# Matmuls on constants in the light slots of a pair-attention stage

## The chip, the cores and the metric

The kernel runs on one core of a Trainium2 chip. Such a core has a matrix engine (TensorE, PE in the profile), VectorE (DVE), ScalarE (ACT) and GpSimd (POOL), and a queue that issues transfers (SyncE, SP). The metric is the time of one execution on the device in microseconds (us); a figure for a kernel is the median of several runs. Lower is better.

## What is computed

Two transformer layers on `x` of shape (4, 1024, 256), in float32, each with adaptive layer norms and gates from a small modulation network. The first layer has an RWKV-like recurrence and a mixture of 8 experts. The second has an attention over all pairs of tokens and a gated feed-forward network. Cut to the attention and the network of the second layer:

```python
q = jnp.einsum('bnc,ac->bna', X, Wq)
k = jnp.einsum('bnc,ac->bna', X, Wk)
Vy = jnp.einsum('bnc,dc->bnd', X, Wy_w) + Wy_b
e = jax.nn.relu(_rho_signed_sqrt(q[:, :, None, :] + k[:, None, :, :]))
scores = jnp.einsum('bija,a->bij', e, Wphi)
m = jnp.max(scores, axis=-1, keepdims=True)
ex = jnp.exp(scores - m)
denom = jnp.sum(ex, axis=-1)
part1 = jnp.einsum('bij,bjc->bic', ex, Vy)
Ew = jnp.einsum('bij,bija->bia', ex, e)
part2 = jnp.einsum('bia,ca->bic', Ew, We_w) + We_b * denom[..., None]
return (part1 + part2) / (denom[..., None] + EPS_DEN)
...
h = jax.nn.silu(_tlin(x, w1_w, w1_s)) * _tlin(x, w2_w, w2_s)
h = jax.nn.gelu(_tlin(h, h1_w, h1_s), approximate=False)
h = jax.nn.gelu(_tlin(h, h2_w, h2_s), approximate=False)
return _tlin(h, w3_w, w3_s)
```

`e` has 4 x 1024 x 1024 x 64 elements: for every pair of tokens 64 roots, which are used twice, once for the scores and once, weighted, for `Ew`.

## The kernel before

The program has two stages. `first_layer` runs the first layer; `pair_attention` runs the second, together with what is left of the first (`first_rest`) and with the feed-forward network. The change is in `pair_attention`.

The attention works on blocks of 32 queries: 128 blocks `n`, 32 for each of the four sequences. A block has 8 pairs of tiles (`p` from 0 to 7); a tile holds 128 x 1024 elements of `e`. A pair goes through these steps:

- `begin(p)` takes a buffer from a ring of 14 (`RING`) and, for some halves, has GpSimd add the query to the keys and cut at zero (L1402, L1407);
- `pair(p)`: VectorE or ScalarE adds the other halves (L1416, L1427), ScalarE takes the root of both (L1428), and TensorE multiplies them by the weights of the scores into the block's bank `sc` (L1432), 8 matmuls on four groups of 32 columns;
- later, when the block's scores are complete, `weigh(p, h)`: VectorE multiplies the roots by the spread exponentials and sums them (L1478). This ends the use of the ring's buffer.

In between, once a block: `top` (the maximum on VectorE, L1442, and two small matmuls, L1445), `exps` (L1449, L1451), `spread` (8 matmuls, two times, L1458) and `turn` (L1465).

The order is written out by hand. The main loop runs over blocks and their 8 pairs; one turn of it is called a slot here. In a slot, VectorE weighs pair `p` of the current block, then `work(ROOM[p])` gives other work a place, and then `begin` and `make` start the pairs 13 or 14 places ahead, until the scores' matmuls of one more pair have been issued. Every engine works its instructions off in the order in which they were issued.

The other work is held in two lists of generators: `tasks` (`finish`, the end of the attention for every four blocks) and `stream` (`first_rest`, then for every 256 tokens `dense`, the feed-forward network; and `prepare`, keys and values of the next sequence). A generator issues a few instructions and yields how many matmuls it has used; the room of a slot, `ROOM[p]`, is 3 to 6. A bare `yield` ends the slot for that list and reports nothing. Steps with a bare `yield` after matmuls are the transposes of `normed` (L943) and `finish` (L1491), and the projections of `prepare` (L988, L1002, L1022, L1025). The matmuls of the feed-forward network (L1263, L1333, L1354) report themselves.

The results of the other work go to two PSUM banks (`bank`, tag `"g"`); `banks[0]` counts the free ones. A bank that VectorE is to read is kept for two slots (`LATE`): `later` notes the reading instruction, `tick` at the beginning of `work` issues it when it is due and frees the bank.

`ident` is a 128 x 128 unit matrix, `pick` a constant of 128 x 512 used by `spread`, and `wsel` holds the scores' weights between columns of zeros; `wsel[:, 0, 0:1]` is a column of zeros. `made` counts the pairs whose scores have been issued, `N` is 128.

Of the kernel before, what the change touches and what calls it, by code (L numbers as in the profile page):

```python
# [14 lines left out]
P = 128  # L15
# [16 lines left out]
PREP = 12  # L32
ROOM = (4, 6, 6, 6, 6, 4, 3, 6)
LATE = 2
ADDS = ('ap', 'pp', 'pp', 'dp', 'pp', 'ap', 'dp', 'ap')
FIRST_ON_SCALAR = 6
LEAD = 2
# [6 lines left out]
@with_exitstack  # L44
def block_kernel(ctx: ExitStack, tc: tile.TileContext, a, out):
    nc = tc.nc
    keep = ctx.enter_context(tc.tile_pool(name="keep", bufs=1))


    kept = ctx.enter_context(tc.tile_pool(name="kept", bufs=1, space=DRAM))  # L50
    link = {
        "x1": [kept.tile([U, C], F32, tag=f"x1_{j}", name=f"x1_{j}") for j in range(B * T // U)],
        "x2": [kept.tile([FB, C], F32, tag=f"x2_{j}", name=f"x2_{j}") for j in range(B * T // FB)],
        "gates": [kept.tile([1, 2, B, C], F32, tag=f"gates{j}", name=f"gates{j}") for j in range(2)],
        "brow": kept.tile([1, C], F32, tag="brow", name="brow"),
        "yg": kept.tile([P, 4, U], F32, tag="yg", name="yg"),
        "qd": kept.tile([T, 64], F32, tag="qd0", name="qd0"),
        "nd": kept.tile([64, T], F32, tag="nd0", name="nd0"),
        "kd": kept.tile([8, P, T], F32, tag="kd0", name="kd0"),
        "vd": kept.tile([T, C + 1], F32, tag="vd0", name="vd0"),  # L60
    }

    ident = keep.tile([P, P], F32, tag="ident", name="ident")
    nc.scalar.dma_start(ident, a["ident"])
    cols = [keep.tile([P, 6, 2, B], F32, tag=f"mcols{i}", name=f"mcols{i}") for i in range(2)]
    seen = keep.tile([P, NE], F32, tag="seen", name="seen")
    link["qt"] = [keep.tile([P, 64, 8], F32, tag=f"qt{i}", name=f"qt{i}") for i in range(2)]
    link["wsel"] = [keep.tile([P, n], F32, tag=f"wsel{n}", name=f"wsel{n}") for n in (16, 8)]
    nc.gpsimd.memset(seen, 0.0)
    first_layer(tc, a, link, cols, seen, ident)  # L70
    pair_attention(tc, a, link, out, cols, seen, ident)
# [763 lines left out]
def pair_attention(tc, a, link, out, cols_of, seen, ident):  # L835
# [10 lines left out]
    nc = tc.nc  # L846
# [3 lines left out]
    with tc.tile_pool(name="at_k", bufs=1) as pk, tc.tile_pool(name="at_w", bufs=1) as wp, tc.tile_pool(  # L850
# [24 lines left out]
        wsel = wp.tile([P, 8, 48], F32, tag="wsel", name="wsel")  # L875
# [5 lines left out]
        pick = wp.tile([P, 2, 2, P], F32, tag="pick", name="pick")  # L881
# [168 lines left out]
        def used(j, i):  # L1050
            held.pop(j * ALL + i)
# [3 lines left out]
        banks, late = [2], []  # L1055

        def bank(shape, name):
            banks[0] -= 1
            return pg.tile(shape, F32, tag="g", name=name)

        def later(n, f):
            late.append([n, f])

        def tick():
            for x in late:
                x[0] -= 1
            while late and late[0][0] <= 0:
                late.pop(0)[1]()
                banks[0] += 1
# [174 lines left out]
        def gate(j, m):  # L1244
# [9 lines left out]
            scale = fs[:, m : m + 2, 0:1].to_broadcast([P, 2, FB])  # L1254
            later(LATE, lambda: nc.vector.tensor_tensor(to, ps, scale, ALU.mult))
            yield 4
# [22 lines left out]
        def dense(j):  # L1279
# [15 lines left out]
            def up(ps, m):  # L1295
                for h in range(2):
                    g = two[:, 4 + m + h, :] if m < 4 else one[:, m + h, :]
                    nc.vector.scalar_tensor_tensor(
                        one[:, m + h, :], ps[:, h, :], fs[:, m + h, 1:2], g, ALU.mult, ALU.mult
                    )  # L1300

            for m in range(0, 8, 2):
# [4 lines left out]
                if m % 4 == 2:  # L1307
                    used(j, W2 + m // 4)
                later(LATE, lambda ps=ps, m=m: up(ps, m))
                yield 4  # L1310
# [3 lines left out]
            for li, base, of, to in ((2, H1, one, two), (3, H2, two, one)):  # L1314

                def hidden(ps, m):
                    nc.vector.tensor_tensor(  # L1317
                        to[:, m : m + 2, :], ps, fs[:, m : m + 2, li : li + 1].to_broadcast([P, 2, FB]), ALU.mult
                    )
# [4 lines left out]
                for m in range(0, 8, 2):  # L1324
# [5 lines left out]
                    for h in range(2):  # L1330
# [7 lines left out]
                        used(j, base + m + h)  # L1338
                    later(LATE, lambda ps=ps, m=m: hidden(ps, m))
                    yield 2  # L1340
# [26 lines left out]

            later(LATE, last)
            yield 2
# [11 lines left out]
        class Block:  # L1381
# [9 lines left out]
            def adder(self, i):  # L1391
                return ADDS[i // 2][i % 2]

# [3 lines left out]
            def begin(self, p):  # L1397
                self.s[p] = ring.tile([P, 2, T], F32, tag="s", name="s")
                mine = [h for h in range(2) if self.n and self.adder(2 * p + h) == "p"]
                for h in mine:  # L1400
                    i = 2 * p + h
                    nc.gpsimd.tensor_scalar(  # L1402
                        self.s[p][:, h, :], kB[self.b][i % 8], 1.0, self.query(i), ALU.mult, ALU.add
                    )
                if mine:
                    both = self.s[p][:, mine[0] : mine[-1] + 1, :]
                    nc.gpsimd.tensor_scalar(both, both, FLT_MAX, 0.0, ALU.min, ALU.max)  # L1407
# [152 lines left out]
        N = B * NB  # L1560
        blocks = {0: Block(0)}
# [4 lines left out]
        def work(room):  # L1566


            tick()
            turns[0] += 1  # L1570
            if issues and turns[0] % 2:
                issues.pop(0)()
            for of in (tasks, stream):
                while of and room > 0:
                    got = next(of[0], self_done)
                    if got is self_done:
                        of.pop(0)
                    elif got is None:
                        break
                    else:  # L1580
                        room -= got

        def begin():
            nonlocal begun
# [29 lines left out]
        for n in range(N):  # L1614
            cur = blocks.pop(n)
            ew = ews[n // 4 % 2]
            if n % 4 == 0:
                exT = p2.tile([P, 4, 2, P], F32, tag="exT", name="exT")
            nxt = n + 1 < N
            if n % NB == PREP and n // NB + 1 < B:  # L1620
                stream.insert(min(1 + (follower() in heads), len(stream)), prepare(n // NB + 1))
            for p in range(8):
                if p == 0:
                    cur.spread(1)
                    cur.turn()
                if p == 2:
                    cur.turned(exT)
                cur.weigh(p, 0, ew)
                if made < 8 * N:
                    blocks[made // 8].adds(made % 8)  # L1630
                cur.weigh(p, 1, ew)
                if nxt and p == 5:
                    blocks[n + 1].top()
                if nxt and p == 6:
                    blocks[n + 1].exps()
                    blocks[n + 1].spread(0)
                work(ROOM[p])
                while begun <= 8 * n + p + ahead[0]:
                    begin()
                    make()  # L1640
            if n % 4 == 3:
                tasks.append(finish(n, ew, exT))
        while tasks or stream:
            work(16)
            switch()
# [101 lines left out]
```

## Time and profile before

| | us |
|---|---|
| median of 3 runs | 4834.72 |
| lowest and highest run | 4834.62, 4846.67 |
| profiled execution, whole time | 4844.85 |
| its span, first to last instruction | 4843.1 |
| first score matmul of the attention | 1092 |
| last score matmul of the attention | 4668 |
| mean granted TensorE clock | 0.915 of full |

The span is the time between the first and the last instruction of the profiled execution; 1.75 us lie around it. A page of the profile gives for every group of equal instructions the line, the engine, what is written and read, the shape and the count, then the busy time and the mean duration of one, then the idle time just ahead of them and what ended most of it. The row of the granted clock shows, in 40 slices of the span, how fast TensorE was allowed to run, in tenths. Views of a stretch show the busy time of the engines between two times, and the list of waits shows who waited for whom: total, times, longest. ACT's and DVE's rows are one record for one instruction; a float32 matmul shows as two records.

### The profile page before, as it was taken

The numbers are of one execution on the slowest core, as the hardware profiler recorded it, in microseconds if no ns is written. First come the engines' busy times: TensorE is split into PE (matmuls) and PEld (weight loads), VectorE is DVE, ScalarE is ACT, GpSimd is POOL, SyncE is SP. The second block draws the span as 40 slices with busy tenths as digits, with TensorE's granted clock in tenths as the row PEclk, the third lists the DMA queues.
The fourth block names the chain that finished last, engine by engine and source line by source line (L and its number), as shares of the span: only waits on it lengthen the run. The fifth ranks groups of instructions, "written<-read, shape, count | busy, mean of one in ns | idle before, by whom it ended". The sixth has DMA issues, their size and how long they took to land. (4 is left out here: it accounts for less than half of the span.)

```text
span 4843.1 us, 76620 instructions
## 1 busy us (share of the span) xinstructions
PE 4253.5 (88%) x28714; PEld 2423.4 (50%) x28714; DVE 3881.2 (80%) x6834; ACT 3316.7 (68%) x3183; POOL 3573.9 (74%) x2942
## 2 busy tenths in 40 slices
PE   6899999986888889899897889898889899998888
PEld 1233333433335446555564556555446555555567
DVE  5899999767898888778877878878788878878771
ACT  2333233227888898778878878888788888878851
POOL 3544444337899898889888888888898888888840
PEclk8799999987889889999998999999899999999999
DMA  4344333441112123322222332222223322222223
GB/s 137 91 120 118 107 112 108 128 140 34 33 63 68 63 73 102 105 93 81 79 86 56 109 108 83 85 79 81 66 82 105 106 86 83 77 77 75 78 86 116
DMA packets 256965, 433.16 MB, mean 89 GB/s; under 512 B 71897, under 2 KB 142737, under 8 KB 256337
## 3 DMA queue, kind: packets, MB, share of 16 engines
q1 hardware_dynamic: 253520, 425.76, 28.3%
q8 instruction: 226, 3.70, 0.3%
q10 hardware_dynamic: 2880, 1.98, 0.1%
q14 instruction: 147, 1.20, 0.1%
q0 software_dynamic: 192, 0.52, 0.0%
HBM read 403.99 MB, written 40.93 MB: 92 GB/s over the span
## 5 line engine op out<-in xcount | busy, mean ns | idle before, releaser
L1478 DVE CUSTOM_DVE_ANT_0 s<-s,xb 128x1024 f32<-128x1024 f32 x2048 | 2393.1, 1213 | 63.9 <-PE xb L1458 47.1
L1428 ACT ACTIVATE s<-s 128x2048 f32<-128x2048 f32 x1024 | 1928.6, 1908 | 174.1 <-POOL s L1407 104.6
L1402 POOL TENSOR_SCALAR s<-kB,qt 128x1024 f32<-128x1024 f32 x1397 | 1600.0, 1151 | 281.8 <-DVE ew L1478 108.4
L1407 POOL TENSOR_SCALAR s<-s 128x1024 f32<-128x1024 f32 x1016 | 1421.4, 1399 | 89.1
L1432 PE MATMUL sc<-s,wsel 128*32 128x256 f32 x16384 | 1169.6, 411 | 332.8 <-ACT s L1428 331.6
L1333 PE MATMUL ff_ps<-wide,fw 128*128 128x256 f32 x4096 | 999.1, 393 | 25.1 <-ACT wide L1375 23.7
L1432 PEld LDWEIGHTS sc<-s,wsel 128*32 128x32 f32 x16384 | 456.7, 114 | 903.2 <-ACT s L1428 500.4
L1333 PEld LDWEIGHTS ff_ps<-wide,fw 128*128 128x128 f32 x4096 | 762.8, 193 | 231.3 <-issue 102.5
L741 POOL TENSOR_TENSOR kv<-vb,out_k 128x512 f32<-128x512 f32 x256 | 324.0, 1274 | 244.0 <-DVE state L809 167.4
L1427 ACT ACTIVATE s<-kB,qt 128x1024 f32<-128x1024 f32 x387 | 439.9, 1137 | 18.6 <-DMA kB<-kd 18.1
L616 PE MATMUL e_ps<-wd,hid 128*128 128x512 f32 x896 | 417.8, 613 | 7.0 <-DVE acc L599 4.5
L1458 PE MATMUL xb<-ex,pick 64*128 64x256 f32 x2048 | 320.8, 436 | 46.2 <-ACT ex L1451 46.0
L809 DVE TENSOR_TENSOR_SCAN state<-dec,carry,kv 128x512 f32<-128x512 f32 x256 | 326.2, 1274 | 23.4 <-ACT dec L796 17.5
L616 PEld LDWEIGHTS e_ps<-wd,hid 128*128 128x128 f32 x896 | 170.9, 196 | 233.1 <-issue 219.2
L1416 DVE TENSOR_SCALAR s<-kB,qt 128x1024 f32<-128x1024 f32 x264 | 285.9, 1085 | 0.0
L1263 PE MATMUL ff_ps<-wide,fw 128*128 128x256 f32 x1024 | 268.0, 411 | 17.7 <-DMA fw<-in_ffw_dram 17.0
L1458 PEld LDWEIGHTS xb<-ex,pick 64*128 64x128 f32 x2048 | 193.2, 204 | 180.2 <-ACT ex L1451 80.0
L1317 DVE TENSOR_TENSOR wide<-ff_ps,ffn_s 128x512 f32<-128x512 f32 x128 | 88.0, 687 | 212.2 <-PE ff_ps L1333 212.2
L1442 DVE TENSOR_REDUCE sc<-sc 128x1 f32<-128x256 f32 x128 | 55.1, 431 | 249.0 <-PE sc L1432 248.4
L801 ACT COPY carry<-state 128x1 f32<-128x1 f32 x255 | 47.9, 188 | 295.6 <-DVE state L809 295.3
L1263 PEld LDWEIGHTS ff_ps<-wide,fw 128*128 128x128 f32 x1024 | 200.2, 204 | 79.7 <-issue 35.9
L1451 ACT ACTIVATE ex<-sc,neg 128x256 f32<-128x256 f32 x128 | 60.7, 474 | 254.0 <-DVE neg L1449 252.6
(254 smaller groups left out, 4155.1 us busy)
## 6 DMA issues: line engine op xcount, KB each, us to landing
fw<-in_ffw_dram SPq DMA_DIRECT2D x361, 512.0 KB
vb<-vd SPq DMA_DIRECT2D x1024, 64.0 KB
lent<-vd SPq DMA_DIRECT2D x64, 514.0 KB
wd<-in_w_down_dram SPq DMA_DIRECT2D x28, 1024.0 KB
kB<-kd SPq DMA_DIRECT2D x32, 512.0 KB
lent<-in_We_dram SPq DMA_DIRECT2D x32, 512.0 KB
kd<-nd SPq DMA_DIRECT2D x24, 512.0 KB
vd<-out_v SPq DMA_DIRECT2D x8, 512.0 KB
```

Of the source, the lines that this page charges most:

```text
L616: nc.tensor.matmul(ps, hid[:, k, t * P : (t + 1) * P], wd[:, k, :], start=k == 0, stop=k == HID // P - 1)
L741: nc.gpsimd.tensor_mul(kv, vb[:, g % 2, :], ready[u]["k"][:, n // HN, :])
L809: nc.vector.tensor_tensor_scan(s[:, 1 : U + 1], dec, kv, c, ALU.mult, ALU.add)
L1263: nc.tensor.matmul(ps[:, h, :], w[:, k, o : o + P], hT[:, k, :], start=k == 0, stop=k == 1)
L1333: nc.tensor.matmul(ps[:, h, :], w[:, k * P : (k + 1) * P], of[:, k, :], start=k == 0, stop=k == 7)
L1402: nc.gpsimd.tensor_scalar(self.s[p][:, h, :], kB[self.b][i % 8], 1.0, self.query(i), ALU.mult, ALU.add)
L1407: nc.gpsimd.tensor_scalar(both, both, FLT_MAX, 0.0, ALU.min, ALU.max)
L1427: nc.scalar.activation(t[:, h, :], kB[self.b][i % 8], AF.Relu, bias=self.query(i))
L1428: nc.scalar.activation(t, t, AF.Sqrt, bias=EPS_RHO)
L1432: nc.tensor.matmul(self.sc[32 * j : 32 * j + 32, 0:256], wsel[:, g, 16 * (1 - s) : 16 * (1 - s) + 32], t[:, h, 256 * j : 256 * (j + 1)], s ...
L1458: nc.tensor.matmul(xb[:, 256 * j : 256 * (j + 1)], pick[q, j % 2, s, :], self.ex[q, :], start=True, stop=True)
L1478: nc.vector.tensor_tensor_reduce(t[:, h, :], t[:, h, :], self.xb[s], 1.0, 0.0, ALU.mult, ALU.add, ew[:, self.n % 4, col : col + 1])
```

## The change

A constant `LEAST = 2` is added. `work` notes at its start how much room would be left after two matmuls. After the other work has had its turn, if less than two matmuls were reported, and scores are still to be made, it issues as many matmuls as are missing:

- with a free bank, into this bank: unit matrix times 256 columns of `pick`; the result is not read, and the bank is free again at once;
- without one, into the bank of the block whose scores are being made, if at least one of its pairs has been issued: unit matrix times zeros, added to the scores;
- without either, none.

They stand in TensorE's order after the other work of the slot and ahead of the next pair's scores. The result of the kernel is the same.

```diff
 LATE = 2
+LEAST = 2
 ADDS = ('ap', 'pp', 'pp', 'dp', 'pp', 'ap', 'dp', 'ap')
...
         def work(room):
 
 
+            least = room - LEAST
             tick()
             turns[0] += 1
...
                     else:
                         room -= got
+            if made < 8 * N and room > least:
+                rhs = pick.rearrange("p j s m -> p (j s m)")[:, 0:256]
+                if banks[0]:
+                    ps = bank([P, 256], "idle")
+                    for _ in range(room - least):
+                        nc.tensor.matmul(ps, ident, rhs, start=True, stop=True)
+                    banks[0] += 1
+                elif made % 8:
+                    nothing = wsel[:, 0, 0:1].to_broadcast([P, 256])
+                    for _ in range(room - least):
+                        nc.tensor.matmul(blocks[made // 8].sc[:, 0:256], ident, nothing, start=False, stop=False)
```

## The prediction, made before the changed kernel was run

> **What bounds the kernel now.** I read the page first (span, shares, the row of the granted clock, the costliest groups).
>
> ```profile
> span 4843.1 us, 76620 instructions
> ...
> PE 4253.5 (88%) x28714; PEld 2423.4 (50%) x28714; DVE 3881.2 (80%) x6834; ACT 3316.7 (68%) x3183; POOL 3573.9 (74%) x2942
> ...
> PEclk8799999987889889999998999999899999999999
> ...
> L1432 PE MATMUL sc<-s,wsel 128*32 128x256 f32 x16384 | 1169.6, 411 | 332.8 <-ACT s L1428 331.6
> L1333 PE MATMUL ff_ps<-wide,fw 128*128 128x256 f32 x4096 | 999.1, 393 | 25.1 <-ACT wide L1375 23.7
> ```
>
> No engine is full over the span, and the clock stands at 0.9 or below in many slices. L1432 shows 16384 records for 8192 matmuls in the code: a float32 matmul is two records. The change acts in the pair attention only, from 1092 us (first score matmul) to 4668 us (last). So I took that stretch by itself, then its waits, first VectorE's and then TensorE's.
>
> ```profile
> 1092.00:4668.00 3576.00, 3123.26 (x25366) 1902.67 (x25365) 2940.76 (x5334) 2979.99 (x2258) 3102.59 (x2528) 0.91 0.25 79
> ```
>
> ```profile
> DVE sc L1442 <- PE sc L1432: 248.4, 78, 8.6
> DVE wide L1317 <- PE ff_ps L1333: 119.3, 41, 5.4
> DVE neg L1449 <- PE sc L1445: 82.9, 68, 8.8
> ```
>
> ```profile
> PE sc L1432 <- ACT s L1428: 331.6, 211, 8.4
> ```
>
> The columns of the stretch are PE, PEld, DVE, ACT, POOL busy. VectorE idles 3576 - 2941 = 635 us, and 590 us of that, summed over all its waits in the stretch, ends on TensorE. TensorE idles 453 us (3576 - 3123), 332 of it for ScalarE's roots. So neither runs alone: in heavy slots TensorE is behind and VectorE waits; in light ones TensorE catches up and then starves. One heavy place (TensorE, then VectorE's wait):
>
> ```profile
> 2643.16 1.07 PE L1432 MATMUL sc<-s,wsel 128*32 128x256 f32 x16
> 2644.16 1.13 PE L1022 MATMUL vy_ps<-lent,wide 128*128 128x256 f32 x4
> 2645.22 0.69 PE L1025 MATMUL vy_ps<-lent,part 1*128 1x256 f32 x2
> 2645.85 1.13 PE L1022 MATMUL vy_ps<-lent,wide 128*128 128x256 f32 x4
> 2646.91 0.69 PE L1025 MATMUL vy_ps<-lent,part 1*128 1x256 f32 x2
> 2647.53 1.07 PE L1432 MATMUL sc<-s,wsel 128*32 128x256 f32 x16
> ```
>
> ```profile
> 2653.11 0.43 DVE L1442 TENSOR_REDUCE sc<-sc 128x1 f32<-128x256 f32 x1 [8.59 <-PE sc L1432]
> ```
>
> TensorE goes without a gap, 4.37 us from pair to pair, and VectorE pays 8.59 us at the block's maximum.
>
> **The clock.** TensorE's busy time in stretches of 3.4 us, with the granted clock next to it:
>
> ```profile
> 2583.50:2587.00 3.50, 3.25 (x34) 0.99 0.00 0
> 2587.00:2590.40 3.40, 1.06 (x16) 0.99 0.00 0
> 2590.40:2593.80 3.40, 2.40 (x21) 0.50 0.00 0
> 2597.20:2600.60 3.40, 1.16 (x16) 0.50 0.00 0
> ```
>
> After a stretch with one score pair alone (1.06 of 3.4 us) the clock is 0.50, and the pair then takes 1.93 us instead of 1.07. Over all such stretches of this stage: of 865 at full clock 89 were followed by half clock, and 81 of the 89 had a busy share under 0.48; of the 776 not followed by it only 6 did. Half clock lasts 614 us of the 3576, but VectorE's waits on TensorE lie in it for 93 us only. The other 497 us are at full clock: a backlog of work, which no clock removes.
>
> The Trainium skill, "TensorE: Matmul & The Clock Gate", section "Why this matters for your kernels", warns of idle gaps over about 3 us between bursts. This trace is stricter: the drop above follows a longest gap of 2.59 us. By the page's rule, only the 22 gaps of the stage over 3.41 us could matter, most added matmuls would keep nothing awake, and the sum below would stand near 4,950 us (an estimate from that rule).
>
> **The change, part by part.** It removes and moves nothing: in the built order the sequences of VectorE, ScalarE, GpSimd and SP are as long as before (6568, 2666, 2764 and 551 rows), no DMA is added, and no queue is passed. On TensorE it adds 368 groups of two matmuls, 315 into a spare bank and 53 adding zeros to the scores. Each stands just before a pair's score matmuls.
>
> *Price of a group.* Shape 128x256 with 128 columns of weights, as L1333. Twelve such records stand from 2504.44 to 2507.22 us, 0.232 us each; a group is four records, 0.93 us. A row with poorer weight loading, the two records of L1025 in 0.63 us, would make it 1.26. I take 0.93, the same shape. 368 x 0.93 = 342 us more TensorE work.
>
> *Where it falls.* I gave each group the pair behind it and read TensorE's idle time ahead of that pair in the trace. 125 groups have 0.93 us or more, 43 have 0.15 to 0.93, and 200 have none. So 140 us go into idle time on the spot, and 202 us push the work behind them. The cause: the code counts what steps report in `yield`, not matmuls. In 69 of the groups the slot already carries matmuls that report nothing (L943, L988, L1002, L1022, L1491). Seven such groups lie between 2626 and 2652 us, six of them on top of the heavy slots shown. Another 151 are in truly empty slots that TensorE enters late.
>
> *What reaches the end.* I walked the trace: each group adds 0.93 us of lateness, each idle time of TensorE takes off its own length, and each VectorE wait ended by TensorE turns what is left into delay. 222 us vanish in later idle time, and 121 us become longer VectorE waits, in 100 places. Bounds: 0, if the 453 us of idle took all; 202, if everything without idle on the spot counted. I take 121, since the walk decides it place by place. The cover is TensorE's wait for ScalarE; without it, all 342 us would show.
>
> *What the clock gives back.* Adding the groups' time to the 89 low stretches lifts 52 over 0.48; they lead 382 of the 614 us at half clock. TensorE's busy time there is twice what full clock needs, an excess of 147 us. The same walk with the sign turned (credit lost where TensorE idles anyway, used where VectorE waits on it) leaves 61 us. Bounds: 0, and 93, all of VectorE's waits in half clock. I take 61.
>
> *Bank waits.* The bank must be free: 83 of the groups' first matmuls wait for a VectorE reader, 27 for a ScalarE one. Behind a waiting group stand the next score pair and all of TensorE; VectorE's maximum (L1442) waits for that. Where TensorE is late the reader is done; where it is early it would idle anyway. I take 0; the other end is 83 times one eviction (L1317, 0.69 us): 57 us.
>
> *Sum.* +121 - 61 = +60 us. The profiled execution, 4844.85 us (span 4843.1 and 1.75 around it), would become 4905; it lies 10.1 us over the median of the runs, 4834.72, so the forecast is 4895 us.
>
> **The rivals.** One: it gets faster. The groups fall into idle time and the clock stays up. For it: 125 groups have full cover, and 52 stretches should be mended. It decides if fewer than 66 of the 368 groups' time ends on the path (61 / 0.93); with none, 4834.7 - 61 = 4774, at best 4742 with 93. Against it: 200 groups without cover, and the 497 us of waits at full clock. Chance 0.15. Two: cost and gain meet within 0.3% (14.5 us, about what a measurement of this kernel can tell from no change), 4820 to 4849; about two thirds of the walk's delay would have to be slack. Chance 0.10. Three: the clock is not held, that is, it doesn't do what it is meant to: 4834.7 + 121 = 4956. For it: 32 low stretches have no group in them, and pairs come irregularly against fixed stretches. Against it: 1.07 + 0.93 = 2.0 of 3.4 us is 0.59, over 0.48. Chance 0.12. Four: bank waits stop TensorE's queue: 4895 + 57 = 4952. Against it: the readers are issued before. Chance 0.08.
>
> **How the numbers follow.** The forecast (15 to 105 us slower) has 0.55. Slower in all: 0.55 + 0.12 + 0.08 = 0.75; same 0.10; faster 0.15. The likeliest case's own range is 4850 to 4940. The range to hold 8 in 10 takes in no change below and a clock that isn't held above: 4822 to 4957.
>
> **What would show it.** Right: TensorE's busy time in the attention up by 150 us or more; half clock in it down from 614 to about 250 us, and the mean clock up from 0.91; its wait for ScalarE at L1432 down by half from 332 us; VectorE's waits at the maximum (248 us) and on evictions up although the clock is better; longest around the key projections (L1022). First layer (to 1092 us) and tail (after 4668) unchanged. Wrong: VectorE's waits on TensorE falling under 590 us, which means that lateness is swallowed and the clock's gain stays; half clock near 614 us, which means rival three; added matmuls shown waiting for VectorE by tens of us, which means rival four.

## The result, and the profile after

The changed kernel takes 4912.60 us (median of 4 runs, 4907.74 to 4922.57) against 4840.69 us of the kernel before (4 runs, 4834.62 to 4846.71): ratio 1.0151, 95% interval 1.0132 to 1.0171, so 72 us slower. The profiled execution took 4908.31 us.

The page of the kernel after, the rows that answer to those of before (line numbers are one higher up to L1566; the added matmuls are L1589 into a bank and L1594 as zeros):

```profile
span 4906.5 us, 79572 instructions
...
PE 4488.6 (91%) x30186; PEld 2597.7 (53%) x30186; DVE 3873.9 (79%) x6834; ACT 3315.7 (68%) x3183; POOL 3576.2 (73%) x2942
...
PEclk8799999988999999999999999999999999999999
...
L1433 PE MATMUL sc<-s,wsel 128*32 128x256 f32 x16384 | 1125.1, 394 | 202.9 <-ACT s L1429 202.4
L1334 PE MATMUL ff_ps<-wide,fw 128*128 128x256 f32 x4096 | 984.4, 389 | 32.3 <-ACT wide L1376 30.9
...
L1589 PE MATMUL idle<-pick,ident 128*128 128x256 f32 x1260 | 361.2, 410 | 0.5 <-ACT ewt L1499 0.2
```

The clock's row reads 9 from the eleventh slice on; before, six of those slices read 8. (A 9 stands for 0.9 or more, not for 0.9 or below, as the prediction had it.) A record of the scores takes 394 ns on average instead of 411. So the clock is held, and yet the span is 63 us longer. VectorE, ScalarE and GpSimd have the same work in the same number of instructions.

The attention by itself, 1087 to 4733 us (columns as before: length, busy time of PE, PEld, DVE, ACT, POOL, clock, DMA share, GB/s):

```profile
1087.00:4733.00 3646.00, 3361.79 (x26838) 2079.43 (x26836) 2933.10 (x5335) 2978.55 (x2258) 3104.74 (x2528) 0.97 0.25 78
```

It is 70 us longer (3646 against 3576), so the whole difference lies in it: up to its first score matmul the execution is 4.6 us shorter, and after the last weighing 1.7 us shorter (146.9 against 148.6). TensorE is busy for 238 us more, the clock is 0.97 instead of 0.91, and half clock lasts 215 us instead of 614. VectorE has less busy time in a longer stretch: it waits.

VectorE's longest waits in that stretch, then TensorE's longest (total, times, longest):

```profile
DVE sc L1443 <- PE sc L1433: 300.5, 95, 14.9
DVE wide L1318 <- PE ff_ps L1334: 111.6, 41, 4.2
DVE neg L1450 <- PE sc L1446: 83.3, 67, 8.0
DVE wide L1299 <- PE ff_ps L1264: 56.6, 25, 5.2
```

```profile
PE sc L1433 <- ACT s L1429: 202.4, 133, 6.2
```

VectorE's wait at the block's maximum went from 248.4 to 300.5 us and the one for the second input product (L1299, before L1298) from 29.5 to 56.6. All its waits on TensorE together are 667.7 us in 290 places, before 590.0 in 268: 78 us more, about what the attention grew. TensorE's own wait for roots fell from 331.6 to 202.4 us. So the added work seems to have taken idle time where it lay and to have made VectorE wait where none lay; the experiments test this.

The heavy place that the prediction showed, in the kernel after: the same two pairs on TensorE, then VectorE's wait at the same maximum (start, duration):

```profile
2671.60 1.07 PE L1433 MATMUL sc<-s,wsel 128*32 128x256 f32 x16
2672.61 1.13 PE L1023 MATMUL vy_ps<-lent,wide 128*128 128x256 f32 x4
2673.66 0.69 PE L1026 MATMUL vy_ps<-lent,part 1*128 1x256 f32 x2
2674.29 1.13 PE L1023 MATMUL vy_ps<-lent,wide 128*128 128x256 f32 x4
2675.35 0.69 PE L1026 MATMUL vy_ps<-lent,part 1*128 1x256 f32 x2
2675.97 1.13 PE L1589 MATMUL idle<-pick,ident 128*128 128x256 f32 x4
2677.03 1.07 PE L1433 MATMUL sc<-s,wsel 128*32 128x256 f32 x16
```

```profile
2683.67 0.43 DVE L1443 TENSOR_REDUCE sc<-sc 128x1 f32<-128x256 f32 x1 [14.95 <-PE sc L1433]
```

From pair to pair it is now 5.43 us (2671.60 to 2677.03), before 4.37: the added group lies on top of six matmuls of projections that report nothing. Seven groups stand between 2650 and 2682 us ahead of this maximum, and VectorE waits there for 14.95 us instead of 8.59: 6.4 us more, six groups' time.

### The profile page after: what moved, and what is told of

The parts are those of the page before. It is cut to its first block, busy times and chain, and to the rows that moved or that the text cites. A ratio compares the mean times of both kernels' runs of the same rounds, so it can differ in the third digit from the quotient of the medians.

```text
span 4906.5 us, 79572 instructions
## 1 busy us (share of the span) xinstructions
PE 4488.6 (91%) x30186; PEld 2597.7 (53%) x30186; DVE 3873.9 (79%) x6834; ACT 3315.7 (68%) x3183; POOL 3576.2 (73%) x2942
## 5 line engine op out<-in xcount | busy, mean ns | idle before, releaser
L1433 PE MATMUL sc<-s,wsel 128*32 128x256 f32 x16384 | 1125.1, 394 | 202.9 <-ACT s L1429 202.4
L1334 PE MATMUL ff_ps<-wide,fw 128*128 128x256 f32 x4096 | 984.4, 389 | 32.3 <-ACT wide L1376 30.9
L1334 PEld LDWEIGHTS ff_ps<-wide,fw 128*128 128x128 f32 x4096 | 752.4, 191 | 231.8 <-issue 100.0
L1433 PEld LDWEIGHTS sc<-s,wsel 128*32 128x32 f32 x16384 | 434.5, 111 | 758.1 <-ACT s L1429 323.2
L1589 PE MATMUL idle<-pick,ident 128*128 128x256 f32 x1260 | 361.2, 410 | 0.5 <-ACT ewt L1499 0.2
L1459 PE MATMUL xb<-ex,pick 64*128 64x256 f32 x2048 | 295.3, 408 | 11.9 <-ACT ex L1452 11.6
L1264 PE MATMUL ff_ps<-wide,fw 128*128 128x256 f32 x1024 | 267.4, 410 | 14.9 <-DMA fw<-in_ffw_dram 14.1
L1589 PEld LDWEIGHTS idle<-pick,ident 128*128 128x128 f32 x1260 | 220.6, 195 | 109.8 <-issue 80.7
L1459 PEld LDWEIGHTS xb<-ex,pick 64*128 64x128 f32 x2048 | 179.1, 189 | 133.5 <-issue 57.9
```

What stands on the lines that cost most here:

```text
L1334: nc.tensor.matmul(ps[:, h, :], w[:, k * P : (k + 1) * P], of[:, k, :], start=k == 0, stop=k == 7)
L1433: nc.tensor.matmul(self.sc[32 * j : 32 * j + 32, 0:256], wsel[:, g, 16 * (1 - s) : 16 * (1 - s) + 32], t[:, h, 256 * j : 256 * (j + 1)], s ...
L1459: nc.tensor.matmul(xb[:, 256 * j : 256 * (j + 1)], pick[q, j % 2, s, :], self.ex[q, :], start=True, stop=True)
L1589: nc.tensor.matmul(ps, ident, rhs, start=True, stop=True)
```

## The experiments

Three questions: is it lateness that costs; is it the banks; and what is the clock worth. For each kernel I read from its trace, besides the time, the half clock in the attention and the *pushed* time: the part of the added matmuls' time in which the root of the pair behind them was already there, so that they stood in front of ready work. Matmuls overlap in TensorE's pipeline; time in which an added one overlaps its neighbours is not counted. In the kernel after the 368 groups take some 360 us of TensorE's time (0.98 each), 257 of them push for 0.4 us or more, and 242 us are pushed.

**Only the places with idle time, and only those without.** The same code, let through for a written list of pairs: the 125 with 0.93 us or more of idle time ahead of them before, or the 200 with none.

```diff
-            if made < 8 * N and room > least:
+            if made in PLACES and made < 8 * N and room > least:
```

> Added matmuls only at the 125 places where the trace of before shows TensorE idle for 0.93 us or more. Lateness theory (cost where TensorE has no idle time, gain from the clock): cost 26, gain 60 us by the walk through the trace, so 34 us faster than before, about 4806 us; half clock in the attention falls from 614 to about 250 us. Rival 1 (the clock is worth nothing): 26 us slower, 4867. Rival 2 (the cost is the wait for a bank, the same at every place): 125/368 of the measured 72 us, 24 us slower, 4865.

> Added matmuls only at the 200 places where the trace of before shows no idle time of TensorE. Lateness theory: cost 78, gain 8 us, so 70 us slower than before, about 4910, the whole loss of the change. Rival 1 (the clock is worth nothing): 78 us slower, half clock as before. Rival 2 (waits for a bank, the same at every place): 200/368 of 72 us, 39 us slower, 4879.

Measured: idle places 4847.63 us against 4840.01 (ratio 1.0016, 1.0006 to 1.0027), 5 us pushed; late places 4907.43 (1.0141, 1.0119 to 1.0164), 192 us pushed. The late places alone are +67 of the +72 us (70 were expected); the idle ones cost 8 us, and the two make up the change (the 43 places with less idle time are in neither). That settles where the loss is made. But the first expectation, 34 us faster, fell: the idle places brought half clock down from 614 to 382 us, and the kernel gained nothing by it. The late places brought it down too, to 413 us.

**Without the 69 filled slots, and with other doses.** First the list turned round: no matmuls in the slots whose projections and transposes report nothing. Then the constant alone: one matmul or four in place of two.

```diff
-            if made < 8 * N and room > least:
+            if made not in PLACES and made < 8 * N and room > least:
```

```diff
-LEAST = 2
+LEAST = 1
```

> The change without the 69 places whose slot already carries two or more matmuls that report nothing; 299 remain. Lateness theory: cost 84, gain 51 us by the walk, so 33 us slower than before, about 4873, and VectorE's long waits around the key projections go back to those of before. Rival 1 (the clock is worth nothing): 84 us slower, 4924. Rival 2 (waits for a bank): 299/368 of 72 us, 59 us slower, 4899.

> One matmul is made up for instead of two (LEAST = 1): the same 368 places, half the TensorE work. Lateness theory: cost 53, gain 42 us by the walk, so 11 us slower than before, about 4852; half clock in the attention about 330 us. Rival 1 (the clock is worth nothing): 53 us slower, 4893. Rival 2 (waits for a bank, one for each place): as slow as the change, 72 us, 4912.

> Up to four matmuls are made up for (LEAST = 4): 1526 added matmuls in place of 736. Lateness theory: cost grows faster than the count because less idle time is left to swallow it; at the 368 places alone 367 less 80 us by the walk, so 170 to 290 us slower than before, 5010 to 5130. Rival 2 (waits for a bank, by the place): below 120 us. Rival 3 (a group costs its own TensorE time wherever it is): 1526/736 of 72 us, 149 us slower, 4989.

Measured: without the filled slots 4888.79 us (1.0099, 1.0084 to 1.0114), 187 us pushed; with one matmul 4872.90 (1.0067, 1.0052 to 1.0082), 110 us pushed; with four 5011.76 against 4835.89 (1.0363, 1.0348 to 1.0379), 616 us pushed. The filled slots cost 23 us of the 72 (27 were expected of them, from 60 to 33), and without them VectorE's longest wait at a maximum is 8.8 us, as before, instead of 14.9. But the first two are slower than the lateness theory said (49 us against 33, and 33 against 11), though faster than rival 1 said (84 and 53): its gain from the clock was too large here as well. With four matmuls half clock is down to 51 us, the clock is all but full, and the kernel is slowest of all; its 176 us lie at the lower end of the 170 to 290.

**Are the banks to blame?** No bank is asked for; 309 groups add zeros to the scores (59 places have neither).

```diff
-                if banks[0]:
+                if False:
```

> Every group adds zeros to the block's scores and none goes to a bank, so no added matmul waits for a bank; 309 groups. Lateness theory: 309/368 of 72 us, 60 us slower than before, 4900. Rival 2 (the cost is the wait for a bank): the cost is gone and only the clock's gain is left, 4820 or less.

Measured: 4916.01 us against 4835.89 (1.0172, 1.0155 to 1.0189), 203 us pushed. Without one bank touched it is as slow. That is 80 us, 20 more than its theory said; why is not shown. The kernel after says the same of the banks: its row of L1589 above has 0.5 us of idle time ahead of all the matmuls that go into a bank.

**A cheaper filler.** Six transposes of 128 x 128 in place of two matmuls, at 121 of the idle places and at all 315 places with a bank.

```diff
-                    for _ in range(room - least):
-                        nc.tensor.matmul(ps, ident, rhs, start=True, stop=True)
+                    for k in range(3 * (room - least)):
+                        h = slice(k % 2 * P, k % 2 * P + P)
+                        nc.tensor.transpose(ps[:, h], rhs[:, h], ident)
```

> As the run on the 125 idle places, but each group is six transposes of 128x128 (one record of 0.165 us each by L1465, 0.99 us a group) in place of two matmuls, at the 121 places that have a bank. The Trainium skill says that transposes do not count as activity for the clock. If that holds, half clock stays near 614 us and the run shows the cost without the clock's gain: lateness theory 26 us slower than before, 4866, so the clock is worth 26 less the 8 us measured with matmuls, 18 us. If transposes count, half clock falls to about 380 us as with the matmuls, and the time is that run's, 4848.

> The whole change with six transposes for each group, at the 315 places with a bank; the 53 groups of zeros are left out. If transposes do not count for the clock: half clock near 614 us, lateness costs some 100 us of the 121, 4940, more than the change itself by the clock's worth. If they count: half clock about 230 us and 315/368 of 72 us, 62 us slower, 4902.

Measured: idle places 4842.27 us (1.0016, 1.0006 to 1.0025), half clock 386 us, 3 us pushed; all places 4878.04 (1.0084, 1.0069 to 1.0099), half clock 300 us, 124 us pushed. At the idle places they held the clock as the matmuls did (386 against 382 us) and cost as little: a second filler with the same missing gain. At all places both numbers missed the forecast (about 230 us of half clock, 62 us slower). Six transposes are shorter than two matmuls: where a pair follows at once, it starts 0.80 us after the group (median), with matmuls 1.06.

**What is lost follows what is pushed.** All kernels that fill the light slots or a part of them, each against the kernel before of its own group of runs:

| kernel | half clock us | pushed us | change of time us | per us pushed |
|---|---|---|---|---|
| idle places, transposes | 386 | 3 | +6 | |
| idle places | 382 | 5 | +8 | |
| one matmul | 317 | 110 | +33 | 0.30 |
| all, transposes | 300 | 124 | +42 | 0.34 |
| without filled slots | 239 | 187 | +49 | 0.26 |
| late places | 413 | 192 | +67 | 0.35 |
| zeros only | 287 | 203 | +80 | 0.39 |
| the change | 215 | 242 | +72 | 0.30 |
| four matmuls | 51 | 616 | +176 | 0.29 |

Some 0.3 us (0.26 to 0.39) are lost for each us that stands in front of ready work, with either filler. What the clock gives back is already in these numbers, and it may be part of their spread: the kernel without filled slots and the one with late places push almost the same time (187 and 192 us), and the one with 174 us less of half clock loses 18 us less, 0.10 us per us. Their places differ, so this is a hint and no proof.

**What is the clock worth?** Where did the 232 us of mended half clock go in the kernel with idle places alone? TensorE, that kernel first, then the kernel before at the same work:

```profile
2399.77 1.99 PE L1272 MATMUL ff_ps<-wide,fw 128*128 128x256 f32 x8
2405.25 1.07 PE L1441 MATMUL sc<-s,wsel 128*32 128x256 f32 x16 [3.48 <-ACT s L1437]
2406.25 3.65 PE L1272 MATMUL ff_ps<-wide,fw 128*128 128x256 f32 x8
```

```profile
2398.87 1.65 PE L1432 MATMUL sc<-s,wsel 128*32 128x256 f32 x16 [1.56 <-ACT s L1428]
2400.65 2.08 PE L1458 MATMUL xb<-ex,pick 64*128 64x256 f32 x8
2402.66 1.99 PE L1263 MATMUL ff_ps<-wide,fw 128*128 128x256 f32 x8
2407.19 1.07 PE L1432 MATMUL sc<-s,wsel 128*32 128x256 f32 x16 [2.53 <-ACT s L1428]
2408.19 1.99 PE L1263 MATMUL ff_ps<-wide,fw 128*128 128x256 f32 x8
```

Before, half clock lies on a score pair and a spread (1.65 and 2.08 us) after which TensorE waits anyway. With filler there, TensorE is done sooner, waits 3.48 us for ScalarE instead of 2.53, and the clock lapses at the next product: 3.65 us instead of 1.99, and that one VectorE reads. (That the wait is longer is not the whole reason; see the last section.) Over the attention the score records at half clock fall from 1766 to 844, but those of the feed-forward products rise from 223 to 246, and VectorE's waits for the second input product from 29.5 to 52.4 us. So I filled more of the idle time, and only idle time: all 145 pairs of the main loop with 0.93 us or more, whatever the slot reports, with two or four matmuls (140 of them had a place for these); and 593 matmuls, which went to 171 pairs, as many as the idle time ahead of each holds at 0.465 us. The edit of the second:

```diff
-            if made < 8 * N and room > least:
+            count = COUNTS.get(made, 0)
+            if count:
...
-                    for _ in range(room - least):
+                    for _ in range(count):
```

> Added matmuls ahead of all 145 pairs at which the trace of before shows TensorE idle for 0.93 us or more, also in slots that reported matmuls: two, or four where it idles 1.9 us or more. Theory A (clock lapses moved: on the 125 places the scores left half clock, but the feed-forward matmuls did not, 223 records at half clock before and 246 after, because the long idle times ahead of them got too little or nothing): feed-forward records at half clock fall below 100, and the kernel is 15 to 40 us faster than before, about 4810. Theory B (the clock is worth nothing here, since TensorE waits for ScalarE anyway): within 10 us of before, whatever the clock.

> 593 added matmuls, four fifths of the change's 736, ahead of 176 pairs, as many at each as TensorE's idle time there in the trace of before holds at 0.465 us a matmul. Theory A: 20 to 45 us faster than before, feed-forward records at half clock below 80. Theory B: within 10 us of before. Rival 3 of the last runs (a group costs its own TensorE time wherever it is): 593/736 of 72 us, 58 us slower.

Measured against 4840.68 us: 4829.09 (0.9979, 0.9971 to 0.9988) and 4824.37 (0.9968, 0.9956 to 0.9980), with 11 and 7 us pushed. Half clock is 270 and 215 us, the latter the same as in the kernel after. So 593 matmuls, four fifths of the change's 736, make the kernel 16 us faster when they stand in idle time, and the change's make it 72 slower. But both times, 12 and 16 us faster, lie between Theory B's 10 and Theory A's 15 and 20, and A's mark was missed: 218 and 195 feed-forward records stay at half clock. They stay after idle time that no pair follows: the waits ahead of the spread and of the products behind ScalarE's Gelu. The last experiment fills those too, 102 matmuls ahead of 49 spreads and 73 ahead of 22 products.

```diff
+                    fill(SPREADS.get(n + 1, 0))
                     blocks[n + 1].spread(0)
...
                     ps = bank([P, 2, FB], "ff_ps")
+                    rouse(ps[:, 0, :], HIDDEN.get((j, li), 0) if m == 0 else 0)
...
             ps = bank([P, 2, C], "out_ps")
+            rouse(ps[:, 0, :], HIDDEN.get((j, 4), 0))
```

`fill` and `rouse` issue as many of the added matmuls as their number says; `SPREADS` and `HIDDEN` are written lists.

> The 593 matmuls of the kernel that fills idle time ahead of pairs, and 175 more in the idle time that its trace still shows: 102 ahead of the first spread of 46 blocks (25 waits of 0.93 us or more there, 59.6 us in all) and 73 ahead of the first matmul of a hidden or last product of the feed-forward network (22 waits of 1.15 to 2.29 us for ScalarE's Gelu, 38 us). Open is why the clock is worth so little: 400 us of half clock mended there brought 16 us. Theory A: the mended part lay where TensorE starves anyway, and what is left (195 feed-forward records at half clock, each 0.21 us dearer, most of them after these waits) is the part that VectorE waits for. Then half clock falls from 215 us to 120 or less, feed-forward records at half clock to under 90, VectorE's waits on TensorE that lie in half clock from 32 to under 15 us, and the time goes to 28 to 45 us under the kernel before. Theory B: half clock is worth about 0.04 us per us wherever it lies, since a product that comes sooner only makes VectorE wait at its next one. Then the half clock falls just the same and the time stays 13 to 24 us under the kernel before. Third: the new matmuls come late (idle time has moved), some 80 us of TensorE work at 0.29 us per us that stands in front of ready work: up to 23 us lost, and the time is at or over that of the kernel before.

One such place, in the kernel without this filler and in the one with it:

```profile
2530.15 1.13 PE L1474 MATMUL xb<-ex,pick 64*128 64x256 f32 x8 [2.07 <-ACT ex L1467]
2533.37 3.78 PE L1370 MATMUL out_ps<-fw,wide 128*128 128x256 f32 x8 [2.09 <-ACT wide L1391]
2537.08 1.94 PE L1448 MATMUL sc<-s,wsel 128*32 128x256 f32 x16
```

```profile
2522.57 1.99 PE L1606 MATMUL idle<-pick,ident 128*128 128x256 f32 x8
2524.71 1.13 PE L1492 MATMUL xb<-ex,pick 64*128 64x256 f32 x8
2525.78 1.99 PE L1295 MATMUL out_ps<-pick,ident 128*128 128x256 f32 x8
2527.93 1.99 PE L1388 MATMUL out_ps<-fw,wide 128*128 128x256 f32 x8 [0.16 <-ACT wide L1409]
2531.16 1.07 PE L1466 MATMUL sc<-s,wsel 128*32 128x256 f32 x16 [1.23 <-ACT s L1462]
```

The two waits of 2.07 and 2.09 us are full of constants, eight records of the last product take 1.99 us instead of 3.78 and the pair 1.07 instead of 1.94; and then TensorE waits 1.23 us for a root, so part of the 2.7 us goes there.

Measured: 4809.01 us against 4835.98 (0.9941, 0.9927 to 0.9955), 27 us faster, half clock 106 us, feed-forward records at half clock 63, 9 us pushed. Half clock and records fell as both theories said. The time lies between Theory A's 28 to 45 and Theory B's 13 to 24, and A's third mark failed: VectorE's waits that lie in half clock are 37 us, not under 15. The place matters (109 us mended here brought 11 us more, 0.10 per us; the 400 us before them 16, 0.04 per us), but no stretch gives back its excess. It is the fastest kernel here: two matmuls per light slot were not needed for the clock, the idle time held enough.

## Why the prediction was right

The direction and the mechanism of the loss held: +60 forecast, +72 measured, and the loss is made where the prediction put it. That the sum came so near is partly luck. The gain was forecast far too large, the cost probably too large as well, and the two errors nearly cancelled.

- *Price of a group.* 0.93 us forecast, 0.98 measured (360 / 368); 342 us of added work became 360. Behind 295 groups the pair starts at once, and there it starts 1.06 us after the group (median). The forecast took a quarter of twelve records in a row; four on their own are dearer, as its row of L1022 had shown (2644.16 to 2645.22).
- *Where it falls.* 202 us were to push work on the spot; 242 us did. The 200 places without idle time were named (49 of them are filled slots, 151 others), and they are the loss: late places alone +67, all places +72, idle places +8.
- *What reaches the end, +121 us.* The size of this term stays open; it was probably too large. The kernel with its idle time filled shows what 400 us of mended half clock bring without pushed work: 16 us. The last one, with 508 us, shows 27. The change mended 399. With its net of 72, its price is then 88 to 99 us (72 + 16, 72 + 27), some 0.4 us per us pushed, where the walk made 0.6 (121 / 202). By the hint of 0.10 us per us above, the change's 399 us would be worth 40 and the price be 112, near the forecast. That the terms add up so is worked out, not shown: no run pushes work at a fixed clock.
- *What the clock gives back, -61 us.* This is the step that was furthest off. Half clock fell as forecast (614 to 215 us, against "about 250"). But the walk let every us of credit count at VectorE's next wait on TensorE; the runs give 16 to 27, and 40 by the hint above. In the kernel after, VectorE's waits that lie in half clock fell by 23 us only (92.8 to 69.8). With the idle time filled, VectorE's waits in half clock fell from 92.8 to 32.3 us, 60 less, just the forecast's gain, while all its waits on TensorE fell from 590.0 to 569.6, 20 less. So two thirds of it came back as waits at full clock. That this is one bottleneck giving way to the next (TensorE, once ahead, is held by the next root) is shown at the place above; that it is so everywhere is argued.
- *Bank waits, 0.* Right: zeros alone are as slow, and 0.5 us of idle time stands ahead of the matmuls that go into a bank. The rival of 57 us falls.
- *The other rivals.* That the clock is not held falls with 215 us of half clock, and with it the estimate of 4,950 us for the case that most added matmuls keep nothing awake. That cost and gain meet asked for 38 to 62% of the walk's delay to be slack (121 us down to between 75 and 46; the prediction wrote two thirds); with a price of 88 to 112 us it was 7 to 27%. Faster was bound to fewer than 66 groups' time on the path; 242 us, some 247 groups' time, stood in front of ready work, of which about 0.4 counted. The kernels that do meet its condition are 16 and 27 us faster, not 61, and the two that fill the idle places of light slots alone are 6 and 8 us slower.
- *The marks.* TensorE busy in the attention +238 (150 or more forecast), the wait for roots 332 to 202 us (by 39%, half was forecast), waits at the maximum up, the longest around the key projections, first layer and tail as before: these held or came near. Evictions did not all go up: the second input product's did (29.5 to 56.6 us), the hidden products' fell a little (119.3 to 111.6).

## What to carry to other kernels

Before adding work to an engine to keep its clock up, ask at each place whether that engine is waiting there; matmuls in idle time cost almost nothing, and the same matmuls ahead of ready work cost some 0.3 us per us here, after all that the clock returned. Count what the engine really has to do in a slot, not what the code reports. And don't price mended half clock by its excess: look at who waits in it, and then at what that reader waits for next.

## What the runs showed of the hardware

Transposes kept the clock up as well as matmuls at nearly the same places (121 and 125 of them; half clock 386 and 382 us, from 614). The Trainium skill, "TensorE: Matmul & The Clock Gate", section "Part 4: PE-mode transpose", says that they don't count as busy in the same way; for the float32 transposes of this program (one record each, where a float32 matmul has two) the runs don't agree, and they decide.

Lapses move. Filling 125 places took away 232 us of half clock but put 23 more feed-forward records into it. At the place shown two things meet. TensorE, being earlier, waits longer for the next root. And in every trace here the clock changes only on a fixed grid of 3.413 us (118 stretches at half clock in the kernel before, 69 in the kernel after), so it counts where a wait falls on that grid: before, the wait of 2.53 us is cut by a grid line at 2406.04, TensorE is busy for 0.59 and 0.66 of the two cells (stretches between grid lines) beside it, and the clock stays; with filler the wait of 3.48 us lies mostly in one cell, of which TensorE is busy for 0.28, and the next cell is at half clock. That this holds for the other moved lapses is not shown.

A drop needs no long gap. Of the 89 drops in the attention before, 56 follow a grid cell that no idle time of TensorE over 3 us reaches into.
